# Four stacked selective-scan layers on one core: one accumulation across the turn of a direction, finer yields in the side work, and a first prologue split in two

## The chip, the core and the metric

The kernel runs on one core of one Trainium2 chip. Its time is the device time of one execution in microseconds (us); where several executions are given, the median counts. Five engines work side by side, each through its own queue in order: TensorE (PE; its weight loads are listed as PEld), VectorE (DVE), ScalarE (ACT), GpSimd (POOL) and SyncE (SP), which issues all DMAs here.

## The reference

x has shape (8, 48, 48, 96). Four layers are applied one after the other, each as x = x + ss2d(groupnorm(x)). The core of ss2d, cut to what matters:

```python
xc, z = split(x @ in_proj_w.T)              # 192 channels each
xc = silu(depthwise_conv3x3(xc) + conv_b)
xs = stack([x_hw, x_wh, x_hw[..., ::-1], x_wh[..., ::-1]])   # 4 directions, L = 2304
dts, Bs, Cs = split(einsum('bkdl,kcd->bkcl', xs, x_proj_w))
delta = softplus(einsum('bkrl,kdr->bkdl', dts, dt_proj_w) + dt_proj_b)
def step(h, inp):                           # a scan over the 2304 pixels, 16 states n
    dA = exp(d_t[..., None] * A)
    h = dA * h + (d_t * u_t)[..., None] * b_t[:, :, None, :]
    y = einsum('bkdn,bkn->bkd', h, c_t)
# the four directions' y are turned back and summed, + Ds * xs,
# then layernorm over channels, * silu(z), @ out_proj_w.T
```

Layer 3 states its scan with cumulative sums and a decay that fades to zero, so that only the first and last 192 pixels of a direction contribute beyond the skip term; the kernel computes just these ends for it.

## The kernel before

**Tiles.** The eight images are worked in four pairs. A pair has 2 x 192 channels, which are three tiles t of 128 partitions: t=0 and t=1 are the first 128 channels of either image, t=2 the last 64 of both. For each (layer l, pair p) there are 12 groups (t, ph, d): ph 0 walks rows and ph 1 columns, d 0 forward and d 1 backward. Layers 0 to 2 cut a direction of 2304 pixels into three chunks of 768 (class Chunk), 36 chunks per pair. A backward direction takes the three chunks in the opposite order, so the last chunk of d=0 and the first chunk of d=1 cover the same pixels. I call that place the turn; there are six per pair. A chunk has 16 steps, one for each state n. Layer 3 works on the ends alone (class Edge), 4 steps of 4 states per group.

**One step.** ScalarE makes da = exp(a_n * dl) (L712). TensorE spreads row n of B over the partitions into a PSUM tile b (L729, two buffers). VectorE multiplies b by du (L741) and scans h = da * h + b (L745). For every fourth state B comes by DMA and is multiplied on POOL (L684), and ScalarE writes the exponent into the PSUM tile instead. POOL multiplies h by C, which a DMA has broadcast into cb (L754). Four steps later (LAG) `add_up` adds cb into the PSUM tile acc with an identity matmul (L788). acc is two banks wide and has one buffer. At the first step of a chunk `add_up` starts acc with what y already holds (L782: y times the identity, or u times the skip diagonal in the first direction). After the last it hands over `collect`, which copies acc back into y on ScalarE (L803) at the start of the next step, before that step's other work. In ph 1 the copy and the L782 reads go through y with a stride.

**Around the steps.** `prepare` computes the next chunk's softplus dl and du in two halves, in small pieces, one piece a step (L573 on TensorE, L578 to L589 on ScalarE, L591 and L592 on POOL, L595 to L602 on VectorE). The next pair's `prologue` and the last pair's `epilogue` are Python generators, the side work. The main loop in `run` takes one piece (a side step) from one of them after each step, and none in a step that has just collected (`busy`). A piece that yields True says that it still holds a PSUM bank. `side_step` then goes on with that generator; otherwise it takes the one that has made the smaller share of its estimated total. Side work and `prepare` share the tile pool ps, of two one-bank buffers. In layer 3 ten side steps are taken at each step.

**The prologue** of a pair loads the two images, takes the group norm, projects in (L393, L401 on TensorE, L397 and L405 copies on ScalarE), convolves tile t with nine shifted diagonal matmuls per chunk of rows (L301, then L309 on ScalarE, silu at L259), and projects u to dt, B and C (`x_projection`: L454, copies L465 and L467, store to DRAM as xd at L481). `parts_of` fetches B back (L426), splits it into three bf16 parts (L430 to L441 on ScalarE and POOL) and stores it as xb (L445). A chunk reads xb as brow (L692) and xd as dts (L546), cb (L701) and bb (L673). The convolution of tile 1 and 2 waits (GATED) until a third and two thirds of the running pair's steps are done, since it needs a buffer of u.

**Order.** The very first prologue and the first `prepare` run before the loop, and the last epilogue after it. For layers 0 to 2 `keep_order` fixes each engine's order to that of the program, so an instruction that waits holds up all behind it on its engine. The start and layer 3 are ordered by the tile framework's scheduler.

Of the kernel before, what the change touches and what calls it, by code (L numbers as in the profile page):

```python
# [102 lines left out]
def ss2d_layers_kernel(ctx: ExitStack, tc: tile.TileContext, x_in, consts, weights, out):  # L103
# [167 lines left out]

    GATED = "gated"

    def prologue(l, p, short=False):
        ly = layers[l]
        gn = gnpool.tile([DM, 2, 2], F32, name=f"gn_{l}_{p}", tag="gn")
        xd = dram.tile([2, 2, ly.nx, L], F32, name=f"xd_{l}_{p}", tag=f"xd{ly.rank}")
# [10 lines left out]

        def convolve(pad, t):

            while place["tiles"] < t:
                yield GATED
            u[t] = upool.tile([P, L], F32, name=f"u_{l}_{p}_{t}", tag="u")
            for c0, m in CHUNKS:
                r0, nr = c0 // W, m // W
                ps = bank()
                for j in range(9):
                    dy, dx = divmod(j, 3)  # L300
                    nc.tensor.matmul(  # L301
                        ps[:, :m],
                        ly.diag[:, int(t == 2), j, :],
                        pad[:, r0 + dy : r0 + dy + nr, dx : dx + W],
                        start=(j == 0),
                        stop=(j == 8),
                    )
                    yield True
                nc.scalar.activation(  # L309
                    u[t][:, c0 : c0 + m], ps[:, :m], AF.Identity, bias=ly.column(t, C_CONVB)  # L310
                )
            yield
            silu(u[t], u[t])
            yield

# [5 lines left out]
        for b in range(2):  # L321
# [67 lines left out]
            for c0, m in CHUNKS:  # L389
                r0, nr = c0 // W, m // W  # L390
                rows = slice(1 + r0, 1 + r0 + nr)
                ps = bank()
                nc.tensor.matmul(  # L393
                    ps[:, :m], ly.inw[:, 0:P], x[:, c0 : c0 + m], start=True, stop=True
                )
                yield True
                nc.scalar.copy(  # L397
                    pad[:, rows, 1 : W + 1], ps[:, :m].rearrange("p (r w) -> p r w", w=W)
                )
                ps = bank()  # L400
                nc.tensor.matmul(  # L401
                    ps[q0 : q0 + 64, :m], ly.inw[:, P:DIN], x[:, c0 : c0 + m], start=True, stop=True
                )
                yield True
                nc.scalar.copy(  # L405
                    pad2[q0 : q0 + 64, rows, 1 : W + 1],
                    ps[q0 : q0 + 64, :m].rearrange("p (r w) -> p r w", w=W),
                )
            yield
            yield from convolve(pad, b)  # L410
        yield from convolve(pad2, 2)

        steps = {}

        def later(i, held, f, *args):
            steps.setdefault(i, []).append((held, f, args))
# [1 line left out]
        def parts_of(o, ph, b, src, dst, rows, m):  # L420
            got = {}

            def fetch():
                got["raw"] = raw = sm1.tile([P, L // 4], F32, name="raw", tag="raw")
                for d in range(2):
                    nc.sync.dma_start(raw[rows * d : rows * d + rows, :m], src(d))  # L426

            def first():
                got["parts"] = parts = sm1.tile([P, PARTS, L // 4], BF16, name="parts", tag="parts")
                nc.scalar.copy(parts[: 2 * rows, 0, :m], got["raw"][: 2 * rows, :m])  # L430

            def second():
                raw, at = got["raw"], slice(0, 2 * rows)
                nc.gpsimd.tensor_sub(raw[at, :m], raw[at, :m], got["parts"][at, 0, :m])

            def third():
                nc.scalar.copy(got["parts"][: 2 * rows, 1, :m], got["raw"][: 2 * rows, :m])

            def fourth():
                parts, at = got["parts"], slice(0, 2 * rows)  # L440
                nc.gpsimd.tensor_sub(parts[at, 2, :m], got["raw"][at, :m], parts[at, 1, :m])  # L441

            def store():
                for d in range(2):
                    nc.sync.dma_start(dst(d), got["parts"][rows * d : rows * d + rows, :, :m])  # L445

            for i, f in ((0, fetch), (3, first), (4, second), (7, third), (8, fourth), (11, store)):
                later(o + i, False, f)

        def project(ps, ph, b, half, z, o):  # L450
# [4 lines left out]

        def x_projection(i, ph, b):

            o, got = 12 * i, {}

            def put(ps, c0, m):  # L460
                if "xt" not in got:
                    got["xt"] = tmp.tile([ly.nx, L], F32, name=f"xt_{l}_{p}_{ph}_{b}", tag="tmp")
                xt, r0, nr = got["xt"], c0 // W, m // W
                if ph == 0:
                    nc.scalar.copy(xt[:, c0 : c0 + m], ps[: ly.nx, :m])  # L465
                else:
                    nc.scalar.copy(  # L467
                        xt.rearrange("p (w h) -> p h w", h=H)[:, r0 : r0 + nr, :],
                        ps[: ly.nx, :m].rearrange("p (r w) -> p r w", w=W),
                    )  # L470

            def mul(half, c0, m):
                if half == 0:
                    got["ps"] = bank()
                project(got["ps"], ph, b, half, lambda z: z[:, c0 : c0 + m], slice(0, m))

            for j, (c0, m) in enumerate(CHUNKS):
                later(o + 2 * j, True, mul, 0, c0, m)
                later(o + 2 * j + 1, True, mul, 1, c0, m)
                later(o + 2 * j + 2, False, lambda *a: put(got["ps"], *a), c0, m)  # L480
            later(o + 11, False, lambda: nc.sync.dma_start(xd[ph, b], got["xt"]))  # L481
            row = 2 * ly.rank
            parts_of(
                o + 15, ph, b,
                lambda d: xd[ph, b, row + 2 * NS * d : row + 2 * NS * d + NS, :].rearrange(
                    "n (q m) -> (n q) m", q=4
                ),
                lambda d: xb[ph, b, :, d].rearrange("k n (q m) -> (n q) k m", q=4),
                4 * NS, L // 4,
            )  # L490
# [34 lines left out]
                NS, EDGE,  # L525
            )

        for ph in range(2):
            for b in range(2):
                (x_projection_of_ends if short else x_projection)(2 * ph + b, ph, b)  # L530
        for i in range(max(steps) + 1):
            held = False
            for holds, f, args in steps.get(i, ()):
                f(*args)
                held = held or holds
            yield held


    HALF = SCAN // 2
# [100 lines left out]
    class Chunk:  # L640


        def __init__(self, l, p, t, ph, d, i, group):
            self.l, self.p, self.t, self.ph, self.d, self.group = l, p, t, ph, d, group
            self.c0, self.m = SCANS[i if d == 0 else len(SCANS) - 1 - i]
            self.first, self.last = i == 0, i == len(SCANS) - 1
            self.batches = range(2) if t == 2 else (t,)
            self.brow = self.acc = self.dts = None
            self.cb, self.da, self.rq, self.b = {}, {}, {}, {}
# [121 lines left out]

        def add_up(self, n):
            l, t, s = self.l, self.t, state[self.l, self.p]
            if n == 0:
                self.acc = pacc.tile([P, 2, BANK], F32, name="acc", tag="acc")

                if self.ph == self.d == 0:
# [9 lines left out]
            for a in range(2):  # L787
                nc.tensor.matmul(  # L788
                    self.acc[:, a, : self.m // 2], ident, c[:, a, :],
                    start=False, stop=(n == NS - 1),  # L790
                )
            if n == NS - 1:
                late_sums.append(self.collect)

        def collect(self):
# [273 lines left out]
    def side_step(*sides):  # L1069

        for s in sorted(sides, key=lambda s: (not s.held, s.made / s.total)):
            got = next(s.g, s)
            s.held = got is True
            if got is not s and got is not GATED:
                s.made += 1
                return

    marks = []

# [17 lines left out]
    def run(pairs, short):  # L1097


        def units():  # L1100
            for l, p in pairs:
                for gi, (t, ph, d) in enumerate(groups):
# [4 lines left out]
                        continue  # L1107
                    group = {}
                    for i in range(len(SCANS)):
                        c = Chunk(l, p, t, ph, d, i, group)  # L1110
                        for n in range(NS):
                            yield (l, p, (gi * len(SCANS) + i) * NS + n), c, n

        def begin(l, p):
            if l not in layers:
                layers[l] = Layer(l)
            return prologue(l, p, l in short)

        todo = list(units())

# [16 lines left out]
            for i in range(k + DECAYS if k else 1, min(k + DECAYS + 1, len(todo))):  # L1137
                todo[i][1].decay(todo[i][2])

        drain(begin(*pairs[0]))  # L1140
        chunks = list(dict.fromkeys(c for _, c, _ in todo))
        drain(prepare(chunks[0]))
        behind = ahead = Side()
# [4 lines left out]
        for k, ((l, p, unit), c, n) in enumerate(todo):  # L1148
# [5 lines left out]
            all_units = len(groups) * (per if l in short else len(SCANS) * per)  # L1154
            place["tiles"] = 3 * unit // all_units
            if done:
                behind, done = Side(epilogue(*done), 210), None
            if unit == LAG and following:
                ahead = Side(begin(*following), 280)
            if n == 0:  # L1160
                drain(coming)
                if unit + per == all_units:
# [19 lines left out]
            step(coming)  # L1182

            for _ in range(10 if l in short else 0 if busy else 1):
                side_step(behind, ahead)
        for _, c, n in todo[-LAG:]:
            collected()
            c.add_up(n)
# [113 lines left out]
```

## Time and profile before

| what | value |
|---|---|
| median of three runs (lowest to highest) | 21633.64 us (21624.16 to 21662.88) |
| the profiled execution, and its span | 21617.61 us, 21615.8 us |
| mean granted TensorE clock | 0.943 |
| first scan starts, last scan of layer 2 starts | 243.0 us, 19607.8 us |

Busy time by stage, in us (the stretches are: before the first scan, layers 0 to 2, layer 3 with the last epilogue):

| stage | length | PE | DVE | ACT | POOL | clock |
|---|---|---|---|---|---|---|
| 243 to 19608 | 19365 | 17126.6 | 17940.0 | 12075.2 | 17229.0 | 0.95 |
| 19608 to 21616 | 2008 | 1540.0 | 904.5 | 1452.1 | 758.7 | 0.85 |

The span runs from the first to the last instruction. "Idle before, releaser" in the profile is how long an engine stood idle ahead of an instruction and which instruction or DMA ended that. Shares of busy time are means over the stage and say nothing of who waits for whom; the waits do.

### The profile page before, as it was taken

To read this page: it belongs to the slowest core of one execution; us is meant where nothing else is said; L and a number is where in the kernel's file an instruction comes from. 1 tells how busy PE (TensorE), PEld (TensorE's weight loads), DVE (VectorE), ACT (ScalarE), POOL (GpSimd) and SP (SyncE) were. 2 spreads that over 40 slices of the span, in tenths; PEclk is the share of its full clock that TensorE was granted. 3 is DMA by queue.
4 is the path that set the end of the run, shared out by engine and by line. 5 is a ranking of instruction groups with operands and counts; after the bars stand their busy time and mean duration, and the time that the engine had idled before them with its cause. 6 is when DMAs were issued, how large, how long until landed. Compare 5 with 4: busy or idle time off the path is not lost. (4 is left out here: it accounts for less than half of the span.)

```text
span 21615.8 us, 229908 instructions
## 1 busy us (share of the span) xinstructions
PE 18860.1 (87%) x64898; PEld 9267.7 (43%) x64898; DVE 18857.4 (87%) x15938; ACT 13615.2 (63%) x24054; POOL 18001.9 (83%) x11081
## 2 busy tenths in 40 slices
PE   8888988988988988988988988988988988988786
PEld 3333443443443444444444444444444444444555
DVE  5999999999999999999999999999999999996443
ACT  4555665665665666665666666656656655666776
POOL 5988889889898898898898888888888888895442
PEclk9999999999999999999999999999999999998887
DMA  3666666666676676676676666666666566663221
GB/s 125 187 191 190 189 193 192 188 193 190 189 200 190 189 198 189 189 199 186 189 198 190 189 194 188 187 191 190 187 191 189 187 192 186 189 191 105 74 68 52
DMA packets 1707635, 3833.01 MB, mean 177 GB/s; under 512 B 238448, under 2 KB 575216, under 8 KB 1693168
## 3 DMA queue, kind: packets, MB, share of 16 engines
q1 hardware_dynamic: 1706352, 3818.21, 60.6%
q8 instruction: 523, 8.57, 0.2%
q14 instruction: 760, 6.23, 0.1%
HBM read 3665.08 MB, written 152.27 MB: 177 GB/s over the span
## 5 line engine op out<-in xcount | busy, mean ns | idle before, releaser
L788 PE MATMUL acc<-cb,cst 128*128 128x384 f32 x27648 | 10802.0, 520 | 0.0
L754 POOL TENSOR_TENSOR cb<-cb,da 128x768 f32<-128x768 f32 x5184 | 9362.0, 1816 | 1706.4 <-DVE da L745 1047.4
L788 PEld LDWEIGHTS acc<-cb,cst 128*128 128x128 f32 x27648 | 5045.4, 197 | 3982.6 <-issue 1503.7
L745 DVE TENSOR_TENSOR_SCAN da<-da,carry,b 128x768 f32<-128x768 f32 x3456 | 6267.1, 1813 | 219.3 <-DVE b L741 1.8
L741 DVE TENSOR_TENSOR b<-du,b 128x768 f32<-128x768 f32 x5184 | 4915.6, 948 | 966.9 <-PE b L729 960.2
L712 ACT ACTIVATE da<-dl,a 128x768 f32<-128x768 f32 x5184 | 4767.5, 926 | 90.5 <-POOL cb L754 57.9
L729 PE MATMUL b<-brow,pick 48*128 48x512 bf16 (+3 forms) x10368 | 2661.3, 338 | 1629.0 <-DVE da L745 1319.0
L712 ACT ACTIVATE b<-dl,a 128x768 f32<-128x768 f32 x1728 | 1559.8, 903 | 2956.9 <-DVE da L745 2841.7
L754 POOL TENSOR_TENSOR cb<-cb,bb 128x768 f32<-128x768 f32 x1728 | 3137.3, 1816 | 230.4 <-issue 61.6
L684 POOL TENSOR_TENSOR bb<-bb,du 128x768 f32<-128x768 f32 x1728 | 3136.8, 1815 | 131.5 <-DMA bb<-xd 105.3
L745 DVE TENSOR_TENSOR_SCAN da<-da,b 128x768 f32<-128x768 f32 x1728 | 3029.9, 1753 | 109.6 <-ACT b L712 1.9
L729 PEld LDWEIGHTS <-pick 48*128 48x128 bf16 (+1 forms) x10368 | 672.9, 97 | 4467.5 <-DVE da L745 2342.7
L745 DVE TENSOR_TENSOR_SCAN bb<-b,carry,bb 128x768 f32<-128x768 f32 x1152 | 2069.5, 1796 | 21.8 <-ACT b L712 15.2
L301 PE MATMUL ps<-pad,diag 128*128 128x480 f32 (+1 forms) x4320 | 1972.1, 557 | 7.5 <-ACT u L309 5.0
L638 ACT COPY carry<-da 128x1 f32<-128x1 f32 x3456 | 627.1, 181 | 1041.1 <-DVE da L745 1026.0
L578 ACT ACTIVATE ps<-ps,w 128x384 f32<-128x384 f32 (+1 forms) x912 | 497.2, 545 | 1113.0 <-PE ps L573 1111.1
L782 PE MATMUL acc<-y,cst 128*128 128x384 f32 x1296 | 807.3, 755 | 368.0 <-ACT y L803 194.8
L301 PEld LDWEIGHTS ps<-pad,diag 128*128 128x128 f32 x4320 | 800.0, 190 | 723.9 <-issue 310.8
L591 POOL TENSOR_TENSOR lg<-lg,w 128x384 f32<-128x384 f32 (+1 forms) x912 | 894.0, 980 | 224.7 <-ACT w L589 224.7
L745 DVE TENSOR_TENSOR_SCAN bb<-b,bb 128x768 f32<-128x768 f32 x576 | 999.6, 1735 | 34.1 <-ACT b L712 28.5
L592 POOL TENSOR_TENSOR lg<-lg,e 128x384 f32<-128x384 f32 (+1 forms) x912 | 890.5, 976 | 71.2
L573 PE MATMUL ps<-dts,w 6*128 6x384 f32 (+5 forms) x2432 | 814.7, 519 | 149.3 <-DVE du L599 63.9
(141 smaller groups left out, 17513.5 us busy)
## 6 DMA issues: line engine op xcount, KB each, us to landing
cb<-xd SPq DMA_DIRECT2D x4736, 384.0 KB
cb<-xd SPq DMA_DIRECT2D x4736, 192.0 KB
bb<-xd SPq DMA_DIRECT2D x1152, 384.0 KB
bb<-xd SPq DMA_DIRECT2D x1152, 192.0 KB
yd<-y SPq DMA_DIRECT2D x48, 1152.0 KB
ey<-yd SPq DMA_DIRECT2D x256, 216.0 KB
brow<-xb SPq DMA_DIRECT2D x576, 72.0 KB
ex<-xs SPq DMA_DIRECT2D x256, 108.0 KB
```

What stands on the lines that cost most here:

```text
L301: nc.tensor.matmul(ps[:, :m], ly.diag[:, int(t == 2), j, :], pad[:, r0 + dy : r0 + dy + nr, dx : dx + W], start=(j == 0), stop=(j == 8),)
L573: nc.tensor.matmul(o[:, :m], ly.dtw[q0 : q0 + r, k, chans], dts[q0 : q0 + r, at], start=True, stop=True,)
L591: nc.gpsimd.tensor_sub(lg, lg, w1)
L592: nc.gpsimd.tensor_add(lg, lg, e)
L684: nc.gpsimd.tensor_mul(b, b, self.du)
L712: nc.scalar.activation(da, self.dl, AF.Exp, scale=columns_of(self.l, self.t, self.ph, self.d, n))
L729: nc.tensor.matmul(b[:, z : z + zm], w, self.brow[:k, z : z + zm], start=True, stop=True)
L741: nc.vector.tensor_mul(b, self.du, b)
L745: nc.vector.tensor_tensor_scan(way(h), way(da), way(b), start, ALU.mult, ALU.add)
L754: nc.gpsimd.tensor_mul(c, c, h)
L782: nc.tensor.matmul(self.acc[:, a, : self.m // 2], w, self.y_part(z)[:, a], start=True, stop=False,)
L788: nc.tensor.matmul(self.acc[:, a, : self.m // 2], ident, c[:, a, :], start=False, stop=(n == NS - 1),)
```

## The change

Three edits.

1. **One sum at the turn.** A chunk gets `turned`, the chunk before it where d=1 begins, and `turns`, true for the last chunk of d=0. A chunk that turns has no stop flag and no `collect`; the chunk after it takes over the same acc without L782 and adds its 16 states to it. So 72 of 432 collects and 72 of 432 starts of acc are gone, and in those 72 steps `busy` is false.
2. **Yields.** The convolution yields without holding after each chunk of rows, not only at the end. The input projection yields without holding after each copy. `x_projection` takes three steps for each chunk of rows (two products, then the copy by itself) where it took two (the copy in the step of the next product). The estimated totals become 195 for the epilogue (210 before) and 300 for the prologue (280 before). The pieces of `parts_of` have new names only.
3. **The first prologue in two.** With first=True the convolution of tile 1 is left out at first, the gates are off, and only the x_projection for (ph 0, image 0) is made before READY. Then the first `prepare` runs and the loop begins. The rest, which is x_projection (1, 0), the convolution of tile 1 and the projections (0, 1) and (1, 1), is taken as side steps, ahead of any other side work.

```diff
@@ prologue, convolve
-            while place["tiles"] < t:
+            while place["tiles"] < t and not first:
                 yield GATED
...
                     u[t][:, c0 : c0 + m], ps[:, :m], AF.Identity, bias=ly.column(t, C_CONVB)
                 )
-            yield
+                yield
             silu(u[t], u[t])
@@ prologue, input projection
                     pad[:, rows, 1 : W + 1], ps[:, :m].rearrange("p (r w) -> p r w", w=W)
                 )
+                yield
                 ps = bank()
...
-            yield
-            yield from convolve(pad, b)
+                yield
+            if not (first and b == 1):
+                yield from convolve(pad, b)
         yield from convolve(pad2, 2)
@@ x_projection
-            o, got = 12 * i, {}
+            o, got = 15 * i, {}
...
-                later(o + 2 * j, True, mul, 0, c0, m)
-                later(o + 2 * j + 1, True, mul, 1, c0, m)
-                later(o + 2 * j + 2, False, lambda *a: put(got["ps"], *a), c0, m)
-            later(o + 11, False, lambda: nc.sync.dma_start(xd[ph, b], got["xt"]))
+                later(o + 3 * j, True, mul, 0, c0, m)
+                later(o + 3 * j + 1, True, mul, 1, c0, m)
+                later(o + 3 * j + 2, False, lambda *a: put(got["ps"], *a), c0, m)
+            later(o + 15, False, lambda: nc.sync.dma_start(xd[ph, b], got["xt"]))
             row = 2 * ly.rank
             parts_of(
-                o + 15, ph, b,
+                o + 19, ph, b,
@@ prologue, end
+        if first:
+            yield from x_projections((0, 0))
+            yield READY
+            yield from x_projections((1, 0))
+            yield from convolve(pad, 1)
+            yield from x_projections((0, 1), (1, 1))
+        else:
+            yield from x_projections((0, 0), (0, 1), (1, 0), (1, 1))
@@ Chunk
+            self.turned, self.turns = turned, self.last and d == 0
@@ add_up
-            if n == 0:
+            if n == 0 and self.turned:
+                self.acc = self.turned.acc
+            elif n == 0:
                 self.acc = pacc.tile([P, 2, BANK], F32, name="acc", tag="acc")
...
-                    start=False, stop=(n == NS - 1),
+                    start=False, stop=(n == NS - 1 and not self.turns),
                 )
-            if n == NS - 1:
+            if n == NS - 1 and not self.turns:
                 late_sums.append(self.collect)
@@ run
-        drain(begin(*pairs[0]))
+        rest = begin(*pairs[0], first=True)
+        while next(rest) is not READY:
+            pass
+        rest = Side(rest)
...
-                behind, done = Side(epilogue(*done), 210), None
+                behind, done = Side(epilogue(*done), 195), None
             if unit == LAG and following:
-                ahead = Side(begin(*following), 280)
+                ahead = Side(begin(*following), 300)
...
-                side_step(behind, ahead)
+                side_step(rest) or side_step(behind, ahead)
```

`x_projections(*which)` queues the steps of the projections named, issues them in order with a yield after each, and clears the list. `side_step` now returns whether it made a step.

## The prediction

> **What bounds it now.** I read the page's busy times and slices first, then the list of waits of layers 0 to 2 (243 to 19608 us), then the clock record, then timelines of single places.
>
> ```profile
> PE 18860.1 (87%) x64898; PEld 9267.7 (43%) x64898; DVE 18857.4 (87%) x15938; ACT 13615.2 (63%) x24054; POOL 18001.9 (83%) x11081
> ...
> DVE  5999999999999999999999999999999999996443
> ```
>
> VectorE is over 90% busy in 35 slices of 40; the half-idle first slice is the first prologue, the last four are layer 3. Between lie 6912 scans, so one *step* (one state of one chunk) takes (19608 - 243) / 6912 = 2.80 us. The quietest chunk takes 41.2 us for 16 steps, 2.58 each: that is VectorE's own work, and the rest is mostly waiting. The waits of VectorE and of TensorE in that stretch (columns: total us, times, longest):
>
> ```profile
> DVE b L741 <- PE b L729: 960.2, 836, 9.9
> DVE ps L595 <- POOL lg L592: 43.8, 41, 3.8
> ```
>
> ```profile
> PE b L729 <- DVE da L745: 1319.0, 891, 5.1
> PE acc L782 <- ACT y L803: 200.6, 147, 4.4
> PE acc L782 <- ACT carry L638: 197.5, 143, 4.3
> ...
> PE ps L401 <- ACT pad L397: 23.1, 18, 1.6
> PE ps L573 <- DVE du L602: 21.8, 30, 1.7
> PE ps L454 <- ACT xt L467: 19.1, 12, 2.3
> ```
>
> VectorE waits for one thing: the rows of B that TensorE spreads at L729. TensorE waits for VectorE too, so each is late by turns, and a microsecond off TensorE counts only where it is the late one. I numbered the scans 0 to 15 in each chunk and gave VectorE's idle times over 0.15 us to the scan behind them: 1083 us in chunks 1 to 431, of which 495 us stand before scans 5 and 6 and 141 before 7 and 8. A chunk's first add_up comes four steps late, at its scan 4, so this is the change of acc.
>
> **Part 1, one sum at the turn.** One such place, pair 4, t=1, ph=1, on TensorE alone:
>
> ```profile
> 7634.40 0.50 PE L729 MATMUL b<-brow,pick 48*128 48x512 bf16 x2
> 7636.19 2.83 PE L782 MATMUL acc<-y,cst 128*128 128x384 f32 x4 [1.29 <-ACT carry L638]
> 7638.84 2.73 PE L788 MATMUL acc<-cb,cst 128*128 128x384 f32 x4
> 7641.51 0.75 PE L729 MATMUL b<-brow,pick 48*128 48x512 bf16 x2
> ```
>
> The collect (L803, ScalarE, 1.48 us here) must empty the only acc before L782 refills it from y: 1.29 us idle, then 2.83 us of reload. VectorE gets its next B 2.85 us late (its row at 7642.30). The reload is also followed by a slow spell; the clock (the column before the last two):
>
> ```profile
> 7635.00:7638.60 3.60, 2.41 (x4) 1.00 0.35 121
> 7638.70:7642.00 3.30, 3.30 (x7) 0.50 0.01 2
> ```
>
> L788 took 2.73 us where it takes 1.56 at full clock. (The Trainium skill, "TensorE: Matmul & The Clock Gate", Part 1, lets the clock fall to half after an idle window of about 3.4 us. By that rule a 1.29 us gap costs nothing more and the turn would be worth less by that 1.2 us; here half clock follows a gap a third as long, so the row decides.)
>
> The change takes out, 72 times (6 turns in 12 pairs), a collect (mean 0.80 us in ph 0, 1.47 in ph 1), the wait (mean 1.03 and 1.22) and the reload (2.07 and 2.84). What VectorE gets is its idle time there: before scans 5 and 6 of the turn's chunk, 30.0 us over the 36 turns of ph 0 and 75.6 over those of ph 1, 106 together; before scans 7 and 8 another 20.6. Ph 0 is small because TensorE's delay is absorbed there. At the turn's step `busy` is now false, so a side step moves in: at most the 1.0 us of a projection on TensorE, less than the 3 to 4 us removed. I take **-100**; bounds -126 (all of it) and -50 (below).
>
> **Part 2, the bank let go.** Nothing is computed more or less; side steps are spread. Counting yields: a prologue of layers 1 and 2 goes from 248 steps to 291 (three convolutions +4 each, two input projections +9 each, x_projection +13), one of layer 0 from 274 to 317. The epilogue has 195 both ways. Side slots per pair: steps 4 to 559 less about 30, so 527; 512 are needed at most. The gates at steps 192 and 384 leave 167 slots for the last 127 steps and up to 25 of the epilogue: no queue is emptied at once in layers 0 to 2. The gain is TensorE's load per step. In an x_projection each step now carries one product and, each second step, the copy out of the same bank ahead of the next product:
>
> ```profile
> 14438.05 1.03 PE L454 MATMUL ps<-u,w 128*76 128x480 f32 x2 [1.51 <-ACT xt L467]
> 14438.92 0.49 PE L729 MATMUL b<-brow,pick 96*128 96x512 bf16 x2
> ```
>
> TensorE stood 1.51 us for a copy that ScalarE had queued behind the softplus of the next chunk, and VectorE 2.01 us at 14439.45. Per step TensorE has 1.45 to 1.56 (four L788) + 0.37 (0.50 in three steps of four) + 0.11 (two L573 of 0.91 per chunk) + 1.0 = 3.0 us against 2.58 on VectorE. With two products in three steps it is 2.65. In the five chunks that hold the x_projections VectorE idles 15.3 us per pair outside scans 5 and 6, against 1.09 per chunk elsewhere: 15.3 - 5.5 = 9.8, in twelve pairs 118 us. Input projections fall from one product a step to one in two; their 240 steps cost 64 us, 50 above the rate of empty steps. So the most is -168. TensorE's direct waits for banks that go are only 23.1 + 19.1 + a few, 47 us, and the waits of L573 for du (47.1 + 21.8) largely stay, because a convolution holds its bank 9 steps in 10. I take **-70**, nearer the middle; the other bound is +20: about 75 epilogue steps that shift into x_projections of layer 0, at some 0.25 us.
>
> **Part 3, the first scans.** On TensorE, in the first prologue:
>
> ```profile
> 227.16 1.86 PE L573 MATMUL ps<-dts,w 6*128 6x384 f32 x4
> 240.48 1.44 PE L729 MATMUL b<-brow,pick 48*128 48x512 bf16 x4 [11.46 <-DMA brow<-xb]
> 254.97 1.61 PE L573 MATMUL ps<-dts,w 6*128 6x384 f32 x2 [13.05 <-DMA dts<-xd]
> ```
>
> The first scan starts at 243.0. Two convolutions run from 115.79 for 71.47 us; one leaves the path: 35.7. Three x_projections of about 10 us leave it too, but the path then goes through the first one's stores: xd issued at 199.26, raw at 207.47, dts at 208.68, xb at 214.85. Shifted by 35.7, dts is issued at 173; the second dts landed 2.75 us after issue (252.22 to 254.97), and L573 to scan takes 243.0 - 227.2 = 15.8: scan at 192. brow was issued only at 229.99, behind raw and xd transfers of later projections on SP's queue; xb issued at 179, 2.75 (as dts) to 8.2 us (xd to raw) to land, then 2.75 to 10.5 for brow: 185 to 198. So the scan starts at about 195, 48 earlier. The second stop, 9.9 us before 257.37, was SP's issue of dts at 252.22 behind an xb store; that store is now side work: -8. Against it: one convolution and three projections become 128 side steps of pair 0, whose 30 product steps at 0.27 and 45 convolution steps at 0.09 us cost 12. Then pair 0's remaining 317 steps fit 399 slots. **-45**; bounds -60 (nothing paid back) and -25 (brow 10 us later, dts again behind transfers).
>
> **Layer 3** (2008 us, VectorE 45%, TensorE 77%) keeps its work. Its order isn't written out; ten side steps a unit for 40 units meet 438 steps instead of 408, so some 54 instead of 24 are emptied at unit 44. I take **0**, bounds -40 (convolution and epilogue alternate) and +60 (20 us in three pairs).
>
> **Sum.** -100 - 70 - 45 = -215 on the profiled execution's 21617.6: 21402.6. The median shown is 16.0 higher, so I predict **21419**.
>
> **Rivals.**
> 1. *The turn's wait moves on.* Scan 8 is already late in ph 0 (18.2 us over its turns), behind L573 waiting for du. If TensorE stays late until then, part 1 is worth 50: 21469. For it: the side step at the turn. Against: in ph 1 only 2.4 us stand there.
> 2. *The bank wasn't it:* part 2 does not do what it says, if x_projections are late through POOL (parts, about 1.1 us each) and ScalarE: 21489. For it: only 47 us of direct waits. With rival 1 too: 21539. Layer 3 at its worst bound alone: 21479.
> 3. *Slower.* Now a convolution keeps its side from the epilogue; after, some ten of an epilogue's 16 rounds per pair fall between chunks of convolutions and input projections, 110 in eleven pairs. Each has a silu with two table loads, 1.28 + 0.52 + 1.28 = 3.1 us of ScalarE, which can hold a convolution's copy and so its bank. From 215 / 110 = 2.0 us of VectorE each, the change loses; at the full 3.1 it gives 21402.6 + 341 = 21744, 21760 beside the median. Against: all epilogue steps cost VectorE 99 us in 176 rounds, 0.56 each.
>
> **Chances.** Forecast with its own spread 0.58; one of rival 1, rival 2 or layer 3 alone 0.27; two together 0.05; nearly everything given back, 0.06; rival 3, 0.04. About 0.2% (43 us) is what a measurement can tell: faster 0.90, same 0.06, slower 0.04. All best bounds together are -394, all worst +5; leaving out a tenth at each end I take 21310 to 21550.
>
> **What would show it.** First scan near 195 and no 9.9 us stop; L782 x1440 in all instead of 1728 and L803 x360 instead of 432; VectorE's wait for L729 down from 960 to about 780, with scans 5 and 6 of turns empty; half-clock time in layers 0 to 2, 1802 us by the clock record, down by about 100; no L454 behind L467. I am wrong if L729's total falls by less than 80, if long waits for silu stand before L309's readers, or if layer 3's length leaves 1970 to 2070.

## The result, and the profile after

The changed kernel takes 21299.12 us (median of four runs, 21278.81 to 21308.08) where before took 21628.9 (21606.38 to 21662.88): ratio 0.9836, 95% interval 0.9823 to 0.985. I had said 21419 in 21310 to 21550, so it is faster, as forecast, but 11 us below the range. Its profiled execution took 21306.41 us, span 21304.6, against 21617.61. Cut at the first scan and at the last scan of layer 2 (both from the trace), with my own term for each stretch:

| stretch | before | after | measured | forecast |
|---|---|---|---|---|
| to the first scan | 243.0 | 198.9 | -44 | -48 |
| layers 0 to 2 | 19364.8 | 19185.5 | -179 | -100 - 70 - 8 + 12 = -166 |
| layer 3 to the end | 2008.0 | 1920.2 | **-88** | **0** |

Two stretches of three came out within 13 us; what is missing is layer 3. (The sum of the stretches is that of the two profiled executions, 311 us apart; the medians are 330 apart.)

The page's busy times and slices, lines to hold against those of before:

```profile
PE 18651.1 (88%) x64610; PEld 9183.5 (43%) x64610; DVE 18839.5 (88%) x15938; ACT 13518.2 (63%) x23969; POOL 17988.3 (84%) x11081
...
DVE  6999999999999999999999999999999999997453
```

VectorE has the same 15938 instructions and the same busy time; it is the idle time that shrank. TensorE has 288 reloads fewer, ScalarE 72 collects. The waits in layers 0 to 2, VectorE's first, then TensorE's (columns: total us, times, longest; the scan is now L759, the multiply by du L755, the spread L743, the reload L798, the collect L819):

```profile
DVE b L755 <- PE b L743: 780.1, 644, 4.8
```

```profile
PE b L743 <- DVE da L759: 1184.7, 950, 5.7
...
PE ps L454 <- ACT xt L467: 0.7, 1, 0.7
```

The wait for the spread went from 960.2 to 780.1, the longest from 9.9 to 4.8, and the waits for xt from 19.1 to 0.7. VectorE's idle time over 0.15 us in chunks 1 to 431 went from 1083 to 930 us.

The turn shown in the prediction (pair 4, t=1, ph=1), on TensorE:

```profile
7534.46 1.56 PE L804 MATMUL acc<-cb,cst 128*128 128x384 f32 x4
...
7536.93 0.49 PE L743 MATMUL b<-brow,pick 48*128 48x512 bf16 x2
7537.36 2.85 PE L804 MATMUL acc<-cb,cst 128*128 128x384 f32 x8
```

There is no 1.29 us wait and no reload, and the clock stays at 1.00 from 7537.2 to 7540.8. One chunk later, where nothing turns, the old picture is left:

```profile
7581.24 0.50 PE L743 MATMUL b<-brow,pick 48*128 48x512 bf16 x2
7583.04 2.83 PE L798 MATMUL acc<-y,cst 128*128 128x384 f32 x4 [1.30 <-ACT carry L650]
...
7587.85 0.50 PE L743 MATMUL b<-brow,pick 48*128 48x512 bf16 x2
```

Between two spreads lie 6.6 us, and VectorE waits 2.42 us for the second one. The start:

```profile
182.42 2.89 PE L585 MATMUL ps<-dts,w 6*128 6x384 f32 x4 [12.27 <-DMA dts<-xd]
193.58 1.44 PE L743 MATMUL b<-brow,pick 48*128 48x512 bf16 x4 [8.27 <-DMA brow<-xb]
199.20 1.61 PE L585 MATMUL ps<-dts,w 6*128 6x384 f32 x2 [4.18 <-DMA dts<-xd]
```

The wait for the second dts is 4.18 us here instead of 13.05, and no scan stops for it.

**Layer 3.** The first convolution beside the second pair in both traces. Before, on TensorE and then on VectorE:

```profile
20132.45 24.32 PE L301 MATMUL ps<-pad,diag 128*128 128x480 f32 x60
20156.70 0.50 PE L877 MATMUL b<-brow,pick 48*128 48x192 bf16 x4
```

```profile
20157.24 0.96 DVE L882 TENSOR_TENSOR b<-du,b 128x768 f32<-128x768 f32 x1 [17.73 <-PE b L877]
```

After:

```profile
19888.81 7.41 PE L301 MATMUL ps<-pad,diag 128*128 128x480 f32 x18
19896.06 0.65 PE L1018 MATMUL ps<-exn,w 96*128 96x144 f32 x4
...
19903.41 7.44 PE L301 MATMUL ps<-pad,diag 128*128 128x480 f32 x18
```

Layer 3 takes ten side steps at a time, and a convolution that holds its side takes all ten. Here 60 products as the trace counts them, 30 steps, go out in a row, the share of three such takings, so the scheduler that orders layer 3 has also set the spreads of B (L877) behind them; VectorE waits 17.73 us. With the yield, most runs are nine steps long (18 products), and epilogue pieces and spreads come between. The three pairs with a prologue beside them went from 454.2, 466.0 and 473.0 us to 420.9, 437.0 and 440.5; the last pair, which has none, from 608.0 to 610.0.

That wait is one of the longest for the spread, but the waits for the spread do not make the 88 us. VectorE's waits over all of layer 3, before and then after (L883 and L899 wait for ScalarE's exponentials, L595 and L607 for POOL's part of the softplus, L882 and L898 for the spread):

```profile
DVE b L883 <- ACT rq L872: 283.5, 91, 9.7
...
DVE ps L595 <- POOL lg L592: 226.8, 38, 20.4
...
DVE b L882 <- PE b L877: 174.0, 79, 17.9
```

```profile
DVE b L899 <- ACT rq L888: 234.1, 85, 11.2
...
DVE b L898 <- PE b L893: 172.8, 79, 9.0
...
DVE ps L607 <- POOL lg L604: 124.7, 38, 12.0
```

The longest wait for the spread is halved, but their sum is the same; what shrank are the waits for the softplus and for the exponentials, by 102 and 49 us.

### The profile page after: what moved, and what is told of

It is laid out like the page before. It is cut to its first block, busy times and chain, and to the rows that moved or that the text cites. A ratio compares the mean times of both kernels' runs of the same rounds, so it can differ in the third digit from the quotient of the medians.

```text
span 21304.6 us, 229326 instructions
## 1 busy us (share of the span) xinstructions
PE 18651.1 (88%) x64610; PEld 9183.5 (43%) x64610; DVE 18839.5 (88%) x15938; ACT 13518.2 (63%) x23969; POOL 17988.3 (84%) x11081
## 5 line engine op out<-in xcount | busy, mean ns | idle before, releaser
L759 DVE TENSOR_TENSOR_SCAN da<-da,carry,b 128x768 f32<-128x768 f32 x3456 | 6267.3, 1813 | 219.0 <-DVE b L755 1.4
L755 DVE TENSOR_TENSOR b<-du,b 128x768 f32<-128x768 f32 x5184 | 4910.0, 947 | 789.6 <-PE b L743 780.1
L743 PE MATMUL b<-brow,pick 48*128 48x512 bf16 (+3 forms) x10368 | 2660.3, 338 | 1516.2 <-DVE da L759 1184.7
L759 DVE TENSOR_TENSOR_SCAN da<-da,b 128x768 f32<-128x768 f32 x1728 | 3029.5, 1753 | 107.4 <-DVE b L755 0.9
L743 PEld LDWEIGHTS <-pick 48*128 48x128 bf16 (+1 forms) x10368 | 667.2, 97 | 4345.3 <-DVE da L759 2285.7
L759 DVE TENSOR_TENSOR_SCAN bb<-b,carry,bb 128x768 f32<-128x768 f32 x1152 | 2069.7, 1797 | 9.1 <-ACT b L726 6.1
L301 PE MATMUL ps<-pad,diag 128*128 128x480 f32 (+1 forms) x4320 | 1995.8, 560 | 17.0 <-DVE du L611 11.5
L301 PEld LDWEIGHTS ps<-pad,diag 128*128 128x128 f32 x4320 | 807.4, 192 | 721.1 <-issue 293.4
L759 DVE TENSOR_TENSOR_SCAN bb<-b,bb 128x768 f32<-128x768 f32 x576 | 999.2, 1735 | 15.5 <-ACT b L726 11.9
L798 PE MATMUL acc<-y,cst 128*128 128x384 f32 x1008 | 625.3, 751 | 275.2 <-ACT y L819 176.2
```

The source lines that it names most:

```text
L301: nc.tensor.matmul(ps[:, :m], ly.diag[:, int(t == 2), j, :], pad[:, r0 + dy : r0 + dy + nr, dx : dx + W], start=(j == 0), stop=(j == 8),)
L743: nc.tensor.matmul(b[:, z : z + zm], w, self.brow[:k, z : z + zm], start=True, stop=True)
L755: nc.vector.tensor_mul(b, self.du, b)
L759: nc.vector.tensor_tensor_scan(way(h), way(da), way(b), start, ALU.mult, ALU.add)
```

## The experiments

My theory after the result: (A) the turn and the input projection pay as predicted; (B) the convolution's yield, which I gave nothing, makes layer 3 and more, since it lets the epilogue in. The rival: (C) the steps' place does it: each added step moves later side work to other scans of its chunk, and a side step costs by the scan it meets.

"Stalls" are VectorE's idle times over 0.15 us in chunks 1 to 431; "5, 6" those before scans 5 and 6; "X" those before the scan that comes two after a step with products of an x_projection ("behind" such steps, and behind convolution or epilogue steps, is counted in this way below). Times in us; the ratio is to before in the same comparison. Medians and ratios are of several executions, all columns from "first scan" on of the one profiled, which lies between 24 us above its median (e2_first) and 10 below (e10_shift); that of before lies 11 to 40 below the medians of before in the comparisons.

| kernel | median | ratio (95%) | first scan | layers 0-2 | layer 3 | stalls | 5, 6 | X |
|---|---|---|---|---|---|---|---|---|
| before | 21628.9 | 1 | 243.0 | 19364.8 | 2008.0 | 1083 | 495 | 121 |
| e9_before | 21628.2 (one run) | | 244.0 | 19360.8 | 2021.6 | 1081 | 503 | 121 |
| changed, e18_after | 21289.8 | 0.9836 (0.9819-0.9852) | 198.6 | 19181.9 | 1920.5 | 925 | 402 | 91 |
| e1_turn | 21476.6 | 0.9917 (0.99-0.9934) | 275.3 | 19200.2 | 2011.5 | 921 | 375 | 124 |
| e2_first | 21594.1 | 0.9973 (0.9961-0.9984) | 199.5 | 19402.0 | 2014.4 | 1119 | 517 | 127 |
| e3_yields | 21392.0 | 0.9881 (0.9864-0.9897) | 275.8 | 19233.6 | 1886.2 | 971 | 472 | 126 |
| e4_conv | 21339.3 | 0.9851 (0.9835-0.9868) | 274.8 | 19170.1 | 1901.6 | 897 | 471 | 112 |
| e5_conv_held | 21393.1 | 0.9882 (0.9861-0.9902) | 274.9 | 19159.7 | 1966.9 | 888 | 442 | 108 |
| e12_pad | 21519.9 | 0.9941 (0.9924-0.9958) | 274.5 | 19268.5 | 1973.9 | 989 | 517 | 114 |
| e10_shift | 21538.5 | 0.9954 (0.994-0.9968) | 243.4 | 19275.4 | 2007.9 | 1001 | 486 | 74 |
| e6_xproj | 21472.0 | 0.9923 (0.9906-0.9939) | 243.0 | 19220.7 | 2008.0 | 948 | 452 | 39 |
| e11_best | 21252.5 | 0.9818 (0.9801-0.9836) | 198.3 | 19152.6 | 1905.4 | 885 | 400 | 108 |
| e15_held_l3 | 21346.7 | 0.9861 (0.9845-0.9878) | 199.3 | 19175.9 | 1974.7 | 918 | 406 | 90 |
| e13_late | 21162.8 | 0.9779 (0.9762-0.9795) | 198.3 | 19043.1 | 1919.1 | 766 | 53 | 80 |
| e14_best_late | 21282.9 | 0.9837 (0.982-0.9855) | 199.6 | 19178.5 | 1903.8 | 895 | 121 | 147 |
| e16_late_8_10 | 21097.5 | 0.9748 (0.9732-0.9765) | 199.0 | 18987.0 | 1910.8 | 721 | 51 | 82 |
| e17_late_6_9 | **21078.7** | **0.9738 (0.9722-0.9755)** | 198.7 | 18970.9 | 1919.7 | 699 | 55 | 91 |

### The three parts, each alone

e1_turn: `turned`, `turns` and the add_up hunks of the diff, nothing else.

> The kernel before with the first edit alone: one sum at the turn. Theory: VectorE's idle time before scans 5 and 6 of the 72 turn chunks (30.0 + 75.6 us) goes, some 10 to 20 us come back before scans 7 and 8, so layers 0 to 2 get 80 to 110 us shorter; the first scan stays at 243 us and layer 3 stays within 20 us of 2008. Time 85 to 105 us below before. Rival (the wait moves on to scan 8): 50 us or less.

It gave 173. Scans 5 and 6 of the turns went from 105.6 us to 1.9, as foreseen; scans 7 and 8 there only from 20.6 to 25.9, so hardly any of it moved on. Layers 0 to 2 lost 165. The rest, some 60, lies at places that the edit doesn't touch: with `busy` false at turns, side steps fall elsewhere (chunk 30, with the same projections, went from 71 to 27 us of stalls outside scans 5 and 6, over twelve pairs).

e2_first: `first` and READY, with x_projection at two steps as before.

> The kernel before with the third edit alone: the first prologue in two. Theory: the first scan starts at about 199 us instead of 243, the 9.9 us stop behind it goes, and pair 0 pays back 5 to 15 us for the 128 side steps; layer 3 stays within 20 us of 2008. Time 35 to 55 us below before. Rival (the postponed work is paid back in full in pair 0): under 10 us.

56 by the medians (35 to 84 by the interval). The stop of 9.9 us is gone. Pair 0 went from 1600.7 to 1614.0 although it lost that stop: 23 us were paid back where I had 12. By its trace alone nothing is gained: the first scan is 43 us earlier, layers 0 to 2 are 37 and layer 3 is 6 us longer. But that execution is the slowest of its seven, and of the 37 us, 13 lie in pair 0 and the rest in pairs that the edit doesn't touch.

e3_yields: the convolution's, input projection's and x_projection's yields, totals as before. e4_conv: the convolution's alone:

```diff
                     u[t][:, c0 : c0 + m], ps[:, :m], AF.Identity, bias=ly.column(t, C_CONVB)
                 )
-            yield
+                yield
             silu(u[t], u[t])
```

> The kernel before with the yields of the second edit alone (convolution, input projection, x_projection), the estimated totals left at 210 and 280. Theory: layer 3 loses 70 to 100 us of its 2008 as in the whole change, and layers 0 to 2 lose 40 to 80 us, time 110 to 170 us below before. Rival for layer 3 (its gain comes from the new totals or from another edit): layer 3 stays within 25 us of 2008 and the time falls by 40 to 80 us only.

> The kernel before with one yield of the second edit alone: the convolution lets go after each chunk of rows. Theory: this is what shortens layer 3 (the epilogue's small pieces get in between the convolution's matmuls), so layer 3 loses 60 to 90 us and its runs of L301 are 18 matmuls long instead of 60; layers 0 to 2 change by less than 25 us; time 60 to 110 us below before. Rival (the input projection's yields, which double its steps, do it): layer 3 stays within 25 us of 2008.

258 and 310: one line that I had given nothing brings nearly as much as the whole change. It takes 106 us from layer 3 and 195 from layers 0 to 2. The parts aren't additive: 173 + 56 + 258 = 487, the whole change 330 to 358. Nor are the stalls: the turn alone takes away 162 us of them, the yields alone 112, the whole change 153, so in part they remove the same ones. The new totals were not run by themselves.

### The convolution: letting go, a step of its own, or more steps?

e5_conv_held lets the copy have its step but keeps the side; e12_pad only adds as many steps behind the convolution:

```diff
# e5_conv_held
-            yield
+                yield True
             silu(u[t], u[t])
# e12_pad
-            yield
+            for _ in range(5):
+                yield
             silu(u[t], u[t])
```

> Before, with the convolution's copy (L309) in a step of its own, but a held one: as many steps as with the yield that lets go, and the epilogue still shut out from a convolution's first product to its last. The yield that lets go gave 310 us in all, 106 of them in layer 3, whose pairs with a prologue fell from 454, 466, 473 to 415, 434, 435. If letting go is what counts in layer 3, since then convolution and epilogue pieces alternate, those pairs stay at 454 to 473 here and the whole is at most 150 below before. If it is the copy's separate step (the next product no longer queued behind it in one step), the pairs fall as far here and the whole is 250 to 310 below.

> Before, with four more empty steps behind each convolution: the copy L309 stays in the step of the next product and the bank is held as before, but what follows a convolution falls as many steps later as with the copy in a held step of its own. That edit brought layers 0 to 2 from 19365 to 19160, and letting go as well brought no more (19170). If the gain of layers 0 to 2 is a matter of which scans of a chunk the side steps meet, they last 19150 to 19220 here; if it is the copy's own step, they stay at 19270 or above. Layer 3 stays at 2008 within 20 if its gain (2008 to 1967 held, 1902 let go) needs the copy apart and the other side let in.

In layers 0 to 2 letting go is worth nothing (19160 held, 19170 let go): half of theory B falls. Four empty steps give 96 of the 205. The other 109, 55 of it behind convolution steps (stalls 148 to 94), are the copy's own step, or come of the steps standing behind each chunk of rows and not all at the end; these two kernels don't part that. In layer 3 the added steps alone bring 34, held copies 41, letting go 106; two traces of before itself are 14 apart there (2008.0 and 2021.6).

e10_shift moves only the x_projections of layers 0 to 2, four steps later (the text below says layers 1 and 2, but the edit leaves out layer 3 alone, and in the trace those of layer 0 have moved too):

```diff
+        for _ in range(0 if short else 4):
+            yield
         for ph in range(2):
             for b in range(2):
                 (x_projection_of_ends if short else x_projection)(2 * ph + b, ph, b)
```

> Before, with four empty steps ahead of the x_projections of layers 1 and 2 and none in layer 3: nothing is let go earlier, the x_projections and what follows them only fall four steps later in their chunks, as they do with the convolution's yield. With that yield the stalls of chunks 29 and 30 outside scans 5 and 6 went from 125 to 35 us over twelve pairs. If that is a matter of where the steps fall, they fall by 60 to 100 us here, and the time by as much; layer 3 stays at 2008 within 15. If the held bank was the cause, the time stays within 25 us of before.

94 us for steps that do nothing: theory C holds. In before, the stalls of chunk 30 stood at scans 0, 1, 2, 6 and 12, 1.5, 0.9, 0.5, 1.9 and 1.8 us per pair (the mean of pairs 1 to 11); four steps later they are 0.0, 0.0, 0.0, 0.9 and 0.3, and the whole chunk went from 7.5 to 3.2 us. Two stalls of chunk 27 did not move, 2.1 us each on average over the pairs, before scans 3 and 6. They are not the projections': chunk 27 follows a turn, so the second is the reload. Ahead of the first, at 9505.43 us of before's trace, ScalarE makes the silu of the last convolution (2.12 us, with a table load of 1.28 us on either side), and the exponential that the scan needs comes behind it.

e6_xproj has x_projection's three steps alone.

> Before, with the x_projection alone in three steps for each chunk of rows. The prediction had two products in three steps, 2.65 us of TensorE for each step where it had 3.0, take away most of the stalls beside x_projections: by that the stalls behind their product steps fall from 121 us (444 steps) to under 60 and the time by 50 to 90. If the stalls come from where the steps fall, as four empty steps ahead of them alone halved them (121 to 74), they end anywhere from 60 to 140 here, no smaller for the load, and the time is within 60 of before on either side.

The stalls behind its products fell from 121 to 39, below what the shift alone gave (74), and the median by 186, twice the most that I had given. That fits TensorE's load per step, as the prediction had it, but doesn't show it: this edit moves steps as well, and the same three steps show 126 in e3_yields and 91 in the changed kernel, where they meet other scans and other side work.

e11_best leaves out the yields of input projection and x_projection and the new totals.

> Before with the turn, the first prologue in two and the convolution's yield alone; the input projection, x_projection and the totals stay as before. The convolution's yield alone gave 310, with the yields of input projection and x_projection beside it only 258. If those two cost about 50, this is some 30 to 80 below the changed kernel (21220 to 21270). If the 50 came only from where the steps fell in their chunks, it is within 25 us of the changed kernel on either side.

21253, in the range for "they cost about 50". But it was not run beside the changed kernel, whose own median elsewhere is 21290 to 21299, and the intervals of the two ratios overlap; e14_best_late below speaks against leaving them out.

### Layer 3

e15_held_l3 is the changed kernel with one word added, so that only the prologues of layer 3's pairs keep their side:

```diff
-                yield
+                yield short
             silu(u[t], u[t])
```

> The changed kernel, but in the prologues of layer 3's pairs, three of which run beside layer 3, the convolution keeps its side at the copy's step. The work and the number of steps are the changed kernel's. If letting go makes the part of layer 3's gain that the convolution's held copy left out (1967 held against 1902 let go in the kernels with that edit alone), layer 3 goes from 1920 to 1970 to 2000 here, its pairs of 421, 437, 441 to 440 to 460, and the whole is 45 to 80 above the changed kernel. If the copy's own step is enough beside the other yields, layer 3 stays within 15 of 1920. Layers 0 to 2 are 19185 within 30 by both.

Layer 3 is 1974.7, 54 more than in the changed kernel beside it, layers 0 to 2 are 6 us apart, and the whole is 57 slower. VectorE again waits for a spread behind a long run of L301:

```profile
19906.62 20.29 PE L301 MATMUL ps<-pad,diag 128*128 128x480 f32 x50
```

```profile
19929.71 1.83 DVE L898 TENSOR_TENSOR b<-du,b 128x768 f32<-128x768 f32 x2 [10.30 <-PE b L893]
```

So of layer 3's 88 us, 54 are the side let go: one word makes them. Of these, 40 show as VectorE's wait for the spread, which is 213.0 us here and 172.8 in the changed kernel. The remaining 34 are as much as added steps alone gave in e12_pad; that they are the same thing is argued.

What goes with the stretch, though not strictly, is the number of unbroken runs into which the same 810 products of L301 fall there:

| | before | e12_pad | e5_conv_held | e15_held_l3 | e4_conv | changed | e3_yields |
|---|---|---|---|---|---|---|---|
| runs of L301 | 20 | 24 | 23 | 35 | 43 | 45 | 57 |
| layer 3, us | 2008 | 1974 | 1967 | 1975 | 1902 | 1920 | 1886 |

### What the change leaves: the reload at the other boundaries

In the changed kernel 416 us of stalls stand before scans 5 and 6 of chunks that don't turn. e13_late starts the sum with the chunk's first state and adds y's old content later, one bank each time; e16 and e17 do it behind other states.

```diff
-                for a in range(2):
-                    nc.tensor.matmul(
-                        self.acc[:, a, : self.m // 2], w, self.y_part(z)[:, a],
-                        start=True, stop=False,
-                    )
...
-                    start=False, stop=(n == NS - 1 and not self.turns),
+                    start=(n == 0 and not self.turned), stop=(n == NS - 1 and not self.turns),
                 )
+            if n in (4, 8) and not self.turned:
+                a = n // 4 - 1
...
+                nc.tensor.matmul(
+                    self.acc[:, a, : self.m // 2], w, self.y_part(z)[:, a], start=False, stop=False,
+                )
```

> The changed kernel, with the reload of acc (L798) taken out of the step in which acc changes: the sum of a chunk starts with its first state, and what y holds is added one bank behind state 4, the other behind state 8. In the changed kernel 416 us of VectorE's stalls stand before scans 5 and 6 of chunks that are no turn. If they are the reload (2.07 and 2.84 us) on top of the wait for the collect, they fall below 150, and the time by 100 to 250. If they are mostly the wait for the collect, or TensorE gives the half reloads back before scans 10 and 14, the time is within 60 of the changed kernel.

> The same late reload in the kernel with the turn, the first prologue in two and the convolution's yield alone, which was at 21253 where before was at 21633 (ratio 0.9818). Its stalls before scans 5 and 6 are 400 us. If the reload makes them, 21000 to 21150; if the collect's wait does, 21200 to 21310.

> The changed kernel with the late reload, its two halves behind states 8 and 10 in place of 4 and 8. With 4 and 8 the kernel took 21163; 438 us of its stalls stood before scans 8, 9 and 10, where the changed kernel has 183, and the half behind state 8 left nothing behind it (scans 12 to 14: 52). If a reload costs by the scans it meets, these 438 fall to 170 to 230 and the time to 20930 to 21060. If each half costs about the same wherever it is (some 0.7 us), the stalls only move to scans 14 to 16 and the time is 21120 to 21200.

> The same with the halves behind states 6 and 9. If a reload costs by the scans it meets, the stalls before scans 8 to 10 fall to 200 to 300 and the time to 20950 to 21100, near the kernel with 8 and 10. If each half costs the same wherever it is, 21120 to 21200.

> The changed kernel again, as the measure for the three others: 21299 within 25 us, first scan at 199, layers 0 to 2 in 19185 within 20, layer 3 in 1920 within 15.

The stalls before scans 5 and 6 fell from 416 to 53 us: most of them were the reload and not the wait for the collect, which is still there. The non-turning boundary above, in e17_late_6_9 (L794 is its sum):

```profile
7499.47 0.50 PE L743 MATMUL b<-brow,pick 48*128 48x512 bf16 x2
7501.37 1.53 PE L794 MATMUL acc<-cb,cst 128*128 128x384 f32 x4 [1.40 <-ACT carry L650]
7502.83 0.50 PE L743 MATMUL b<-brow,pick 48*128 48x512 bf16 x2
```

1.40 us of wait as before, but 3.4 us between the spreads in place of 6.6. Against the changed kernel beside it e17_late_6_9 is 211 us faster and e16_late_8_10 192, e13_late some 130; VectorE's wait for the spread is

```profile
DVE b L755 <- PE b L743: 543.2, 682, 2.9
```

My numbers for e16 and e17 were half met. The stalls before scan 10 are gone (108 us in e13_late, 4 and 3), those before scans 8 and 9 are not: 343 and 341, against 171 in e18_after, though no reload stands ahead of them. TensorE now waits there for dt projections:

```profile
PE ps L585 <- DVE du L611: 117.2, 76, 2.6
PE ps L585 <- DVE du L614: 116.7, 76, 2.8
```

In the changed kernel those two are 47.4 and 50.2. That they are the cause of scans 8 and 9 is argued, not shown. e14_best_late gained nothing over e11_best: 279 of its 400 us went before scans 5 and 6, and as much came back (X 108 to 147, convolution steps 126 to 254). So the late reload paid beside the finer projections and not without them; that they leave TensorE the room for it is argued.

### The start, once more

> The kernel before, once more, for its own trace. The profiled execution shown first began its scans at 243.0 us; the turn alone, the yields alone and the convolution's yield alone began at 275, though they change nothing ahead of it: from 192 us their 76 products of L454 took 66 us at half clock, where before's went at full clock. If that is a matter of the execution, this trace begins its scans at 275 as well, layers 0 to 2 last the same 19365 within 15 us and the span is near 21648. If it belongs to the edits, it begins at 243 with a span near 21616.

It began at 244.0, as the first trace had; by the terms written down that speaks for the edits, though the turn and the steps behind a convolution change nothing that TensorE runs before 192 us. Four kernels without the split begin at 243 to 244 (before, e9, e10, e6), five at 275 (e1, e3, e4, e5, e12); what decides is open (last section). So the medians of those five carry up to 32 us that their edits need not have made; their stretches in the table don't.

## Where the prediction was right and where it failed

- **The step that failed: "I take 0" for layer 3.** I reasoned that its work stays and that steps are only emptied at unit 44, and gave the alternation of convolution and epilogue at most 40 us. The runs give 88, of which letting go is 54 by e15_held_l3. What I left unread is VectorE's row in layer 3, where it idles 55% of the time: the 17.73 us behind 24.32 us of L301 was in the trace of before. The Trainium skill ("Perfetto Trace Analysis", Optimization Strategy) asks, for the engine that is being worked on, to find its gaps within the stretch in question and what ends each; in this trace the telling gap stood on an engine that was 45% busy. "TensorE 77% busy" hid that held steps in a row keep every other user of TensorE waiting; TensorE's own idle time fell from 468 to 410 us (length less busy time), its busy time from 1540 to 1511. By which waits the 88 us come is open: from before to after VectorE's wait for the spread is the same in total, and those for the softplus and the exponentials fell. With -88 in place of 0 the sum is 21331.
- **Part 1, -100:** right in place and size. The turns' stalls before scans 5 and 6 went from 105.6 to 0. What I did not see is that the edit moves side steps too, which is how I read the further 60 us that it brings when it stands alone.
- **Part 2, -70:** the total of layers 0 to 2 is right (179 against 166), its parts are not. Input projections fell from 64 us to 6, somewhat more than the bound of 50. Behind x_projections the 121 us went to 91; e6_xproj (39) fits the mechanism, but the size depends on where the steps fall. I gave the convolution's yield nothing, since its bank stays held; the bank wasn't the point, but four added steps are worth about 100 alone, and a copy in its own step behind each chunk of rows about 100 more. So that 166 and 179 lie so near is luck: alone, the turn took 165 us from this stretch and the yields 131, where I had 100 and 70, and the two overlap.
- **Part 3, -45:** first scan 198.9 (forecast 195), the 9.9 us stop gone, 23 us instead of 12 paid back (in e2_first).
- **Signs:** the wait for the spread 780.1 (about 780), half-clock time 1802 to 1703 us, by the spells that begin in layers 0 to 2 (down by about 100), L798 1440 times and L819 360, no L454 behind L467 but one of 0.7 us: as listed. Layer 3 left the stretch of 1970 to 2070 that I had named as a sign of being wrong.
- **Rivals:** rival 1 took 20 us (scans 7 and 8 of turns 20.6 to 40.1). Rival 2's price did not come, the stretch lost 179; but its title, that it wasn't the bank, holds for the convolution (19160 held, 19170 let go). Rival 3 did not come: behind epilogue steps VectorE's stalls went from 98 to 74 us.

## What to carry to other kernels

Where side work shares an in-order engine with the main stream, look in every stage for the longest unbroken run of one side and for who waits behind it, above all in stages where several side steps go out at once; a busy share of 77% doesn't show it, and the wait behind the run doesn't price it (174.0 and 172.8 us here for a gain of 88), so break the run and measure. A side step costs by the slot it meets, so try an edit that only shifts the steps (here four empty ones: 94 us) before crediting a gain to a mechanism, and don't add gains of parts that were measured alone. When an accumulator has one buffer, its reload needn't come first: start the sum with new terms and add the old content in a later step; here that brought up to 211 us beside some side work and nothing beside other.

## What the hardware showed unexpectedly

At the start the kernels without the split run the same 76 products of L454 behind the same idle time of 2.40 us on TensorE. The windows behind it (length, PE, PEld, DVE, ACT, POOL, then the granted clock), in before and then in e4_conv:

```profile
191.40:212.00 20.60, 20.38 (x44) 4.65 (x44) 0.00 (x0) 7.86 (x13) 0.50 (x1) 1.00 0.16 57
```

```profile
191.40:212.00 20.60, 20.05 (x24) 4.08 (x24) 0.00 (x0) 5.03 (x8) 0.00 (x0) 0.50 0.06 25
```

The first goes on at full clock, the second at half, for 105.8 us by the clock record although TensorE is busy without a break until 258. The Trainium skill ("TensorE: Matmul & The Clock Gate", Part 1) says that about 3.4 us of sustained work bring the full clock back; here 66 us of products did not, and by that rule the second kernel would have been some 30 us earlier at its first scan (an estimate: these products take 35.9 us in before and 66.1 here). So TensorE's work does not always end such a spell soon, and the same gap does not always begin one: in nine traces, five go on at half clock and four at full. Which it is, and why a kernel shows the same of the two, no run here settles.
